# Layer 0 of a graph network: the first head's mask made earlier, its loads reordered, more layernorm buffers

## The chip, the cores and the metric

The kernel runs on one core of a Trainium2 chip (trn2). A core has five engines that run their own instruction queues: TensorE (PE in the profile; PEld is its weight load), VectorE (DVE), ScalarE (ACT), GpSimd (POOL) and SyncE (SP). They meet through semaphores. SP, ACT and POOL also issue DMAs, each from its own queue. The metric is the device time of one execution in microseconds, as a median of several runs.

## The reference

The network has 4096 nodes with 256 features, a dense 0/1 adjacency matrix, and four layers. Each layer is `x = layernorm(x + layer(x, adj))`. The change lies in layer 0, a graph attention layer with 8 heads of 32 channels:

```python
node_feats = (x @ W.T + b).reshape(num_nodes, num_heads, half)
logit_parent = (node_feats * a[None, :, :half]).sum(axis=-1)
logit_child = (node_feats * a[None, :, half:]).sum(axis=-1)
attn_logits = logit_parent[:, None, :] + logit_child[None, :, :]
attn_logits = jax.nn.leaky_relu(attn_logits, 0.2)
attn_logits = jnp.where(jnp.abs(adj_matrix)[..., None] != 0.0, attn_logits, 0.0)
attn_probs = jax.nn.softmax(attn_logits, axis=1)
out = jnp.einsum('ijh,jhc->ihc', attn_probs, node_feats)
...
x = _layernorm(x + _L0_gnn_ref(x, L0_gnn_W, L0_gnn_b, L0_gnn_a, adj), axis=-1)
```

A pair without an edge keeps logit 0 and so weight 1 in the softmax. Layers 1 to 3 (a product with the adjacency matrix, two steps of a sparsified attention, a mean over neighbours) are not touched by the change.

## The kernel before

The exponential of a leaky logit is a product: exp(p)·exp(c) where parent plus child logit is positive, and exp(0.2p)·exp(0.2c) elsewhere. So layer 0 needs three kinds of sums over the children j of a row i: over the edges with the 0.2 slope, over all nodes that are no edge, and, per head, a correction over those edges whose logit is positive. The first two do not depend on a sign and are one dense product for all heads. The third needs one 0/1 matrix per head.

`sums0` makes the features and the dense product. Its first loop takes pairs of 128-row blocks: it loads `x`, transposes it on PE (L450), copies it to `xT` (L452), multiplies by the weights (L456), and makes the features `nf`, the scaled features `v` and their two-part split `src` on DVE and ACT (L458 to L478). The logits of the parents go to DRAM as `lpd` (L469). `factors0` then finds bounds and writes the row factors `fac` and one integer, `fits`. Three `big` values come back through PE's last small product of that stage, and the PSUM space of the next stage becomes free behind them.

The second loop of `sums0` walks over steps of two row blocks (b = 0, 2, ... 30). In each step eight pieces `a` of the transposed adjacency matrix (2 x 4 blocks of 128x128, 512 KB) are loaded by SP into two buffers (L525). DVE casts a piece to `ar` (L527, two buffers), ACT makes bytes of it, `nb` (L530), which POOL stores to `nad` in DRAM (L531), and PE multiplies `ar` by `src` into `pz` (L537, 256 matmuls in a step). At a step's end DVE combines the sums to `zt`, and ACT issues the store to `zd` (L546 to L552). Between these, `factored` makes for each key block the factors `gb` of the heads, in three bf16 parts that DVE and ACT work out in turn, and stores them to `gmd` (L502 to L514). A scheduler sets the order of all this on each engine; it pulls the factors into the first third of the stage.

`chunk0` belongs to the head stage but is called in step b = 28. It makes the mask `gt0` for the first head and four key blocks over the first 1024 rows, from their stored bytes, with `na0` and `sg0` in the two `a` buffers (L246 to L253). Their factors are loaded to `gm0`.

`choose0` branches on `fits`: a general version of layer 0 follows that does not run on these inputs. All engines meet behind the branch.

The head stage takes two halves of four heads, and in each half four row groups of 1024 rows (`it`). So a head in it is one of 32 passes, each with 256 matmuls (L319): 32 key blocks in eight groups `g` of four, by eight row blocks. For each group a mask `gt` is made by `mask`. In groups 2, 5 and 7 DVE makes four comparisons of the broadcast parent logits `lpb` with a child's logit (L260) and one AND with the adjacency bytes `na` (L262); in the others ACT makes four sign activations (L266) and DVE one shift-and-AND (L268). `sg` has three buffers and `gt` four. At the start of a half SP loads `na` and `gm`, group by group:

```python
for g in range(NB // K):
    nc.sync.dma_start(na[:, g * K:(g + 1) * K], nad[it, :, g * K:(g + 1) * K, :])
    if it == 0 and (half or g):
        nc.sync.dma_start(gm[:, g * K:(g + 1) * K, 0], gmd[half, :, g * K:(g + 1) * K, 0])
```

POOL issues the loads of `lpb` and of `z` (from `zd`). At a head's end DVE reduces `acc` and normalizes it into `y` (L325 to L336). In the second half the row group's result is added to X by POOL (L350, L351), and its four pairs of blocks enter the list `later`. One of them is layernormed with each following head: the moments on DVE (L85, L86), the reciprocal root on POOL (L88, L89) and the last step on POOL too (L96). The pool `work` has two buffers of each tile unless it says otherwise, and so the layernorm's small tiles have two.

Of the kernel before, what the change touches and what calls it, by code (L numbers as in the profile page):

```python
# [9 lines left out]
F32 = mybir.dt.float32  # L10
I32 = mybir.dt.int32
F32R = mybir.dt.float32r
BF16 = mybir.dt.bfloat16
FP8 = mybir.dt.float8e4
U8 = mybir.dt.uint8
# [40 lines left out]
class Net:  # L56
# [17 lines left out]
        self.diag = pool.tile([P, self.NB], F32, name="diag")  # L74
        self.diagr = pool.tile([P, self.NB], F32R, name="diagr")

    def moments(self, pool, src):

        nc = self.nc
        n = src.shape[1]  # L80
        stats = pool.tile([P, n, nc.vector.BN_STATS_DIM], F32, name="ln_stats")
        mv = pool.tile([P, n, nc.vector.BN_AGGR_DIM], F32, name="ln_mv")
        rstd = pool.tile([P, n], F32, name="ln_rstd")
        for q in range(n):
            nc.vector.bn_stats(stats[:, q, :], src[:, q, :])  # L85
            nc.vector.bn_aggr(mv[:, q, :], stats[:, q, :])  # L86
        var = pool.tile([P, n], F32, name="ln_var")
        nc.gpsimd.tensor_scalar_add(var, mv[:, :, 1], EPS)  # L88
        nc.gpsimd.tensor_tensor(rstd, var, self.power.to_broadcast([P, n]), ALU.pow)  # L89
        return mv, rstd  # L90

    def layernorm(self, pool, dst, src, engine=None):

        mv, rstd = self.moments(pool, src)
        for q in range(src.shape[1]):
            (engine or self.nc.vector).tensor_scalar(dst[:, q, :], src[:, q, :], mv[:, q, 0:1], rstd[:, q:q + 1],  # L96
                                                     op0=ALU.subtract, op1=ALU.mult)
# [116 lines left out]
    def layer0(self):  # L214
# [7 lines left out]
        with ExitStack() as ctx:  # L222
# [10 lines left out]
            def row_logits(t, h, it):  # L233
                nc.gpsimd.dma_start(t, bass.AP(tensor=lpd.tensor, offset=lpd.offset + h * N + it * IT, ap=[[0, P], [1, IT]]))
                return t

            first = pool.tile([P, IT], F32, name="lpb0")
            gt0 = pool.tile([P, 4, IT], FP8, name="gt0")
            gm0 = pool.tile([P, 4, 6 * C1], BF16, name="gm0")


            nad = self.nad
# [1 line left out]
            yd = dram.tile([NB, P, D // 2], F32, name="yd")  # L244
            gmd = dram.tile([2, P, NB, H // 2, 6 * C1], BF16, name="gmd")

            def chunk0(work):

                nc.sync.dma_start(gm0, gmd[0, :, 0:4, 0])
                na0, sg0 = (work.tile([P, 2, 4, P], F32, name="a", bufs=2).rearrange("p q k i -> p (q k i)").bitcast(U8)  # L250
                            .rearrange("p (k i) -> p k i", k=4) for _ in range(2))
                nc.sync.dma_start(na0, nad[0, :, 0:4, :])
                mask(gt0, sg0.bitcast(FP8), na0, first, 0, 0)  # L253

            def mask(gt, sg, na, lpb, g, h):

# [11 lines left out]
                    nc.vector.scalar_tensor_tensor(bits[0], bits[1], SIGN_ABOVE, bits[2],  # L268
                                                   op0=ALU.logical_shift_right, op1=ALU.bitwise_and)

            self.sums0(both, nlc, fac, lpd, nad, zd, gmd, lambda: row_logits(first, 0, 0), chunk0)
            self.choose0(fac, zd, gmd, gm0)

            self.open_x()
# [11 lines left out]
            for half in range(2):  # L286
                for it in range(N // IT):
                    i0 = it * Q
                    for g in range(NB // K):
                        nc.sync.dma_start(na[:, g * K:(g + 1) * K], nad[it, :, g * K:(g + 1) * K, :])  # L290
                        if it == 0 and (half or g):
                            nc.sync.dma_start(gm[:, g * K:(g + 1) * K, 0], gmd[half, :, g * K:(g + 1) * K, 0])
                    for hh in range(1, H // 2 if it == 0 else 0):
                        for g in range(0, NB // K, 2):
                            nc.sync.dma_start(gm[:, g * K:(g + 2) * K, hh], gmd[half, :, g * K:(g + 2) * K, hh])
                    if half:
                        nc.sync.dma_start(X[:, i0:i0 + Q, :], xr[:, i0:i0 + Q, :])
                        y0 = work.tile([P, Q, D // 2], F32, name="y0", bufs=1)
                        nc.sync.dma_start(y0, yd[i0:i0 + Q].rearrange("b p d -> p b d"))
                    y = work.tile([P, Q, H // 2, C], F32, name="y")  # L300
                    for hh in range(H // 2):
                        h = half * (H // 2) + hh
                        lpb = row_logits(work.tile([P, IT], F32, name="lpb"), h, it) if h or it else first
                        z = work.tile([P, Q, C1], F32, name="z")
                        nc.gpsimd.dma_start(z, zd[i0:i0 + Q, :, h].rearrange("b p c -> p b c"))
                        acc = psum.tile([P, Q, 256], F32, name="acc")
                        for g in range(NB // K):

                            head0 = half == 0 and hh == 0 and g == 0
                            gt = gt0  # L310
                            if not head0 or it:
                                gt = work.tile([P, K, IT], FP8, name="gt", bufs=4)
                                sg = work.tile([P, K, IT], FP8, name="sg", bufs=3)
                                mask(gt, sg, na[:, g * K:(g + 1) * K, :], lpb, g, h)
                            for k in range(K):
                                jc = g * K + k
                                for q in range(Q):

                                    nc.tensor.matmul(acc[:, q, :6 * C1], gt[:, k, q * P:(q + 1) * P],  # L319
                                                     gm0[:, k, :] if head0 else gm[:, jc, hh, :],  # L320
                                                     start=(jc == 0 and q % 2 == 0),
                                                     stop=(jc == NB - 1 and q % 2 == 1))

                        red = work.tile([P, Q, 2 * C1], F32, name="red")
                        nc.vector.tensor_reduce(red, acc[:, :, :6 * C1].rearrange("p q (s c) -> p q c s", s=3),  # L325
                                                AX.X, ALU.add)

                        red = red.rearrange("p q (s c) -> p q s c", s=2)
                        nc.vector.tensor_mul(red, red, fac[:, 0:2, i0:i0 + Q, h].rearrange("p s q -> p q s").unsqueeze(3)
                                             .to_broadcast([P, Q, 2, C1]))  # L330
                        t1 = red[:, :, 0, :]
                        nc.vector.tensor_add(t1, t1, red[:, :, 1, :])
                        nc.vector.tensor_add(t1, t1, z)
                        r = work.tile([P, Q], F32, name="r")
                        nc.vector.reciprocal(r, t1[:, :, C])
                        nc.vector.tensor_mul(y[:, :, hh, :], t1[:, :, :C], r.unsqueeze(2).to_broadcast([P, Q, C]))  # L336
                        for xs in later[:per_head]:
                            self.layernorm(work, xs, xs, nc.gpsimd)
                        del later[:per_head]
                    y = y.rearrange("p q h c -> p q (h c)")  # L340
                    if not half:
                        nc.gpsimd.dma_start(yd[i0:i0 + Q].rearrange("b p d -> p b d"), y)
                        continue

                    if i0 + Q == NB:
                        self.add_w1()
                    engine = nc.vector if i0 + Q == NB else nc.gpsimd
                    for q in range(0, Q, 2):
                        xs = X[:, i0 + q:i0 + q + 2, :]
                        nc.gpsimd.tensor_add(xs[:, :, :D // 2], xs[:, :, :D // 2], y0[:, q:q + 2])  # L350
                        engine.tensor_add(xs[:, :, D // 2:], xs[:, :, D // 2:], y[:, q:q + 2])  # L351
                        later.append(xs)
# [47 lines left out]
        nc.vector.tensor_reduce(fits, lim.rearrange("p i h -> p (i h)"), AX.X, ALU.min)  # L400
        nc.scalar.dma_start(self.fits, fits)

    def sums0(self, both, nlc, fac, lpd, nad, zd, gmd, then, chunk0):

        nc, tc, NB, D, N = self.nc, self.tc, self.NB, self.D, self.N
        H, C = 8, 32
# [3 lines left out]
        with ExitStack() as ctx:  # L410
# [30 lines left out]
            bb = b0.to_broadcast([P, 2, D + 2 * H])  # L441
            for b in range(0, NB, 2):
                two = slice(b, b + 2)
                x = work.tile([P, 2, D], F32, name="x", bufs=3)
                nc.sync.dma_start(x, xr[:, two, :])
                px = ps.tile([P, 512], F32, name="ps_x", bufs=2)
                for c in range(2):
                    for q in range(2):
# [68 lines left out]
            for b in range(0, NB, 2):  # L517
# [2 lines left out]
                for q in range(2):  # L520
                    factored(b + q)
                for g in range(NB // G):
                    a = work.tile([P, 2, G, P], F32, name="a", bufs=2)
                    for q in range(2):
                        nc.sync.dma_start(a[:, q], self.adjt[b + q, :, g * G:(g + 1) * G, :])  # L525
                    ar = work.tile([P, 2, G, P], F32R, name="ar")
# [5 lines left out]
                    for q in range(2):  # L532
                        for k in range(G):
                            jc = g * G + k
                            for s in range(2):
                                for t in range(2):
                                    nc.tensor.matmul(pz[q][:, t, :W], ar[:, q, k, :], src[:, jc, t, s],  # L537
                                                     start=(jc == 0 and s == 0), stop=(jc == NB - 1 and s == 1))
                if b == NB - 4:
                    chunk0(work)  # L540
                for q in range(2):
                    zt = work.tile([P, 2, H, C1], F32, name="zt")
                    by_head = [t.rearrange("p (h c) -> p h c", h=H) for t in
# [5 lines left out]
                                            op0=ALU.mult, op1=ALU.add)  # L549
                    nc.vector.tensor_mul(zt[:, 1], zt[:, 1], of_row(3))  # L550
                    nc.vector.tensor_add(zt[:, 0], zt[:, 0], zt[:, 1])
                    nc.scalar.dma_start(zd[b + q], zt[:, 0])  # L552

    def general0(self, fac, zd, gmd, gm0):

# [1377 lines left out]
```

## Time and profile before

| what | us |
|---|---|
| median of three runs (4050.99 to 4052.44) | 4052.07 |
| the profiled execution | 4052.79 |
| its span, from the first to the last instruction | 4051.1 |
| opening of layer 0, until the first L537 | 0 to 72.0 |
| dense sums, L537 | 72.0 to 597.1 |
| branch | 597.1 to 602.8 |
| heads, L319 | 602.8 to 1326.5 |
| layers 1 to 3 | from 1326.5 on |

The mean granted clock of TensorE over the span is 0.986. In what follows, a row of the profile's groups reads: line, engine, operation, written tile <- read tiles, shape, count | busy time, mean ns of one | idle time of the engine just before them, and what ended it. A row of waits reads: who <- what ended it: total us, times, longest us. A row of a timeline has start, length, engine, line, operation and tiles, and in brackets the idle time before it with its releaser.

### The profile page before, as it was taken

What the parts mean: (1) busy time and instruction counts of PE and PEld (TensorE: products, weight loads), DVE (VectorE), ACT (ScalarE), POOL (GpSimd) and SP (SyncE); (2) the same over time, 40 slices, a digit from 0 to 9 for tenths busy, and PEclk for the clock granted to TensorE, in tenths of its full rate; (3) what the DMA queues carried; (4) which work ended last, traced back from release to release, by engine and by line L of the source; (5) the groups of instructions that cost most, each with busy time, mean ns of one, the idle gap of its engine ahead of it and who ended that gap; (6) DMA issues with size and microseconds to landing.
All of it is one profiled execution on the core that took longest, in us unless ns stands there. A gap on an engine that the chain in (4) does not pass through costs nothing. (4 is left out here: it accounts for less than half of the span.)

```text
span 4051.1 us, 68763 instructions
## 1 busy us (share of the span) xinstructions
PE 3914.2 (97%) x25081; PEld 3388.4 (84%) x25081; DVE 2994.8 (74%) x6643; ACT 2755.4 (68%) x5127; POOL 1076.8 (27%) x1322
## 2 busy tenths in 40 slices
PE   8999999999999999799999999999999999999899
PEld 7899999999999788468888888864888888888687
DVE  7643228999999444548787887847899999999364
ACT  5543339999998322358888888835888888888132
POOL 0111110111333122301111111113455555555211
PEclk9999999999999999899999999999999999999999
DMA  4765547334221596433233323363333333335541
GB/s 137 230 208 177 179 151 214 96 103 125 70 87 51 222 379 270 121 107 97 95 99 98 103 92 102 105 227 98 105 116 106 103 113 111 103 114 189 185 159 47
DMA packets 322442, 556.42 MB, mean 137 GB/s; under 512 B 72134, under 2 KB 148550, under 8 KB 317990
## 3 DMA queue, kind: packets, MB, share of 16 engines
q1 hardware_dynamic: 239920, 395.13, 30.1%
q0 software_dynamic: 27664, 84.44, 6.2%
q10 hardware_dynamic: 54502, 72.27, 5.2%
q8 instruction: 203, 3.33, 0.3%
q14 instruction: 153, 1.25, 0.1%
HBM read 385.78 MB, written 165.94 MB: 136 GB/s over the span
## 5 line engine op out<-in xcount | busy, mean ns | idle before, releaser
L1334 PE MATMUL ps_a<-X,aT 128*128 128x256 f32 x4096 | 970.5, 380 | 1.3 <-ACT h L1475 1.1
L1334 PEld LDWEIGHTS ps_a<-X,aT 128*128 128x128 f32 x4096 | 776.0, 190 | 125.5 <-issue 3.3
L319 PE MATMUL acc<-gm,gt 128*128 128x198 bf16 x8192 | 706.4, 249 | 23.0 <-DMA gm<-gmd 6.7
L319 PEld LDWEIGHTS <-gt 128*128 128x128 fp8e4 x8192 | 703.1, 98 | 26.3 <-issue 9.3
L266 ACT ACTIVATE sg<-lpb,nlc 128x1024 fp8e4<-128x1024 f32 x636 | 667.2, 1135 | 61.3 <-DVE gt L268 38.6
L179 PE MATMUL ps_r<-XD,adj_piece 128*128 128x512 f32 x1952 | 548.1, 416 | 5.3 <-DMA adj_piece<-adjs 5.2
L537 PE MATMUL pz<-src,ar 128*128 128x264 f32 x4096 | 511.3, 288 | 14.2 <-DVE ar L527 12.2
L537 PEld LDWEIGHTS pz<-src,ar 128*128 128x128 f32 x4096 | 507.7, 190 | 17.7 <-DVE ar L527 11.8
L1061 ACT ACTIVATE ja<-e,nc 128x2048 uint8<-128x2048 f32 x240 | 480.9, 2004 | 2.0
L1327 ACT COPY aT<-ps_tp 128x512 f32<-128x512 f32 x512 | 295.9, 578 | 228.3 <-PE ps_tp L1325 226.4
L179 PEld LDWEIGHTS ps_r<-XD,adj_piece 128*128 128x128 f32 x1952 | 346.1, 190 | 78.9 <-issue 13.4
L530 ACT ACTIVATE nb<-a 128x512 uint8<-128x512 f32 x256 | 156.5, 630 | 288.6 <-DMA a<-in_adjt_dram 279.7
L1126 DVE MAX8 cand<-v 128x8 f32<-128x256 f32 x1024 | 347.1, 411 | 4.4
L1176 DVE SCALAR_TENSOR_TENSOR e<-e,edge 128x512 f32<-128x512 f32 x512 | 347.2, 750 | 2.2
L1325 PE MATMUL ps_tp<-ident,e 128*128 128x128 f32 x2048 | 308.2, 273 | 0.0
L1122 DVE SCALAR_TENSOR_TENSOR v<-e,hi 128x2048 f32<-128x2048 f32 x128 | 301.4, 2355 | 2.4
L1325 PEld LDWEIGHTS ps_tp<-ident,e 128*128 128x128 f32 x2048 | 257.1, 142 | 50.9 <-issue 0.5
L968 PE MATMUL ps_logit<-kT,q 128*128 128x512 f32 x1024 | 278.0, 414 | 12.1 <-DVE kT L926 6.6
L260 DVE TENSOR_SCALAR sg<-lpb,nlc 128x1024 fp8e4<-128x1024 f32 x384 | 285.1, 778 | 5.9 <-DVEq L357 3.9
L970 ACT ACTIVATE e<-ps_logit 128x1024 f32<-128x1024 f32 x256 | 259.8, 1025 | 29.9 <-PE ps_logit L968 28.8
L527 DVE CAST ar<-a 128x1024 fp32r<-128x1024 f32 x128 | 88.6, 693 | 232.9 <-PE pz L537 231.9
L764 PE MATMUL ps_adj<-XD,adj_piece 128*128 128x512 f32 x1024 | 243.5, 398 | 0.0
(383 smaller groups left out, 5497.0 us busy)
## 6 DMA issues: line engine op xcount, KB each, us to landing
adj_piece<-adjs SPq DMA_DIRECT2D x552, 256.0 KB
a<-in_adjt_dram SPq DMA_DIRECT2D x256, 256.0 KB
adjs<-adj_piece SPq DMA_DIRECT2D x96, 512.0 KB
na<-nad SPq DMA_DIRECT2D x64, 512.0 KB
nad<-nb POOLq DMA_DIRECT2D x128, 128.0 KB, 3.4
lpb<-lpd POOLq DMA_DIRECT2D x32, 512.0 KB, 4.0
na<-nad ACTq DMA_DIRECT2D x16, 1024.0 KB
gmd<-gb ACTq DMA_DIRECT2D x64, 198.0 KB
```

Of the source, the lines that this page charges most:

```text
L179: nc.tensor.matmul(ps, a[:, k, :], rhs(jc).rearrange("p s d -> p (s d)"), start=(jc == 0), stop=(jc == self.NB - 1))
L260: nc.vector.tensor_scalar(sg[:, k, :], lpb, nlc[:, 4 * g + k, h:h + 1], 2.0 ** -5, op0=ALU.is_ge, op1=ALU.mult, saturate=False)
L266: nc.scalar.activation(sg[:, k, :], lpb, AF.Sign, scale=-1.0, bias=nlc[:, 4 * g + k, h:h + 1], saturate=False)
L319: nc.tensor.matmul(acc[:, q, :6 * C1], gt[:, k, q * P:(q + 1) * P], gm0[:, k, :] if head0 else gm[:, jc, hh, :], start=(jc == 0 and q % 2 ...
L537: nc.tensor.matmul(pz[q][:, t, :W], ar[:, q, k, :], src[:, jc, t, s], start=(jc == 0 and s == 0), stop=(jc == NB - 1 and s == 1))
L1061: nc.scalar.activation(ja, e[:, s * HALF:(s + 1) * HALF], f, bias=nc1, accum_out=fs[:, i + s:i + s + 1])
L1122: nc.vector.scalar_tensor_tensor(v, ec, hi, ec, op0=ALU.is_lt, op1=ALU.mult, accum_out=sb[:, s:s + 1])
L1126: nc.vector.max(cand[:, 8 * j:8 * j + 8], v[:, k * 256:(k + 1) * 256])
L1176: nc.vector.scalar_tensor_tensor(ec, ec, edge[:, j:j + 1], ec, op0=ALU.is_ge, op1=ALU.mult)
L1325: nc.tensor.transpose(pt[:, k * P:(k + 1) * P], e[:, jc * P:(jc + 1) * P], self.ident)
L1327: nc.scalar.copy(aT, pt)
L1334: nc.tensor.matmul(pa[:, :D], aT[:, k * P:(k + 1) * P], X[:, jc, :], start=(jc == 0), stop=(jc == NB - 1))
```

## The change

The mask of the first head is made for eight key blocks in place of four (`gt0` and `gm0` double), in four parts, each of two key blocks. The parts are called in steps b = 20 to 26; the scheduler, which orders by readiness, puts their instructions where their inputs are ready. Their scratch tiles are those named `nf` and `v`, which the first loop has left. All comparisons are DVE's, and a plain AND follows. For the space, the first loop's x goes through the two `a` buffers, four row blocks at a time. `gt0` is used in the first pass alone (before, its first group of factors also served the later row groups). The loads of `na` and `gm` begin with group 2 and end with groups 0 and 1 in that first row group. The last step's two `zd` stores are issued by SP. The layernorm's four small tiles get six buffers in the head stage.

```diff
-    def moments(self, pool, src):
+    def moments(self, pool, src, bufs=2):
...
-        stats = pool.tile([P, n, nc.vector.BN_STATS_DIM], F32, name="ln_stats")
+        stats = pool.tile([P, n, nc.vector.BN_STATS_DIM], F32, name="ln_stats", bufs=bufs)
...
-            gt0 = pool.tile([P, 4, IT], FP8, name="gt0")
-            gm0 = pool.tile([P, 4, 6 * C1], BF16, name="gm0")
+            gt0 = pool.tile([P, 8, IT], FP8, name="gt0")
+            gm0 = pool.tile([P, 8, 6 * C1], BF16, name="gm0")
...
-            def chunk0(work):
-
-                nc.sync.dma_start(gm0, gmd[0, :, 0:4, 0])
-                na0, sg0 = (work.tile([P, 2, 4, P], F32, name="a", bufs=2).rearrange("p q k i -> p (q k i)").bitcast(U8)
-                            .rearrange("p (k i) -> p k i", k=4) for _ in range(2))
-                nc.sync.dma_start(na0, nad[0, :, 0:4, :])
-                mask(gt0, sg0.bitcast(FP8), na0, first, 0, 0)
+            def early_mask(work, part):
+
+                if part == 0:
+                    nc.sync.dma_start(gm0, gmd[0, :, 0:8, 0])
+                two = slice(2 * part, 2 * part + 2)
+                na0, sg0 = (work.tile([P, 2, H, C1], F32, name=name).rearrange("p s h c -> p (s h c)")[:, :512]
+                            .bitcast(dt).rearrange("p (k i) -> p k i", k=2) for name, dt in (("nf", U8), ("v", FP8)))
+                nc.sync.dma_start(na0, nad[0, :, two, :])
+                for k in range(2):
+                    nc.vector.tensor_scalar(sg0[:, k, :], first, nlc[:, 2 * part + k, 0:1], 2.0 ** -5,
+                                            op0=ALU.is_ge, op1=ALU.mult, saturate=False)
+                bits = [t.rearrange("p k i -> p (k i)").bitcast(U32) for t in (gt0[:, two, :], sg0, na0)]
+                nc.vector.tensor_tensor(*bits, ALU.bitwise_and)
...
-                    for g in range(NB // K):
+                    begun = 2 if it == half == 0 else 0
+                    for g in [*range(begun, NB // K), *range(begun)]:
                         nc.sync.dma_start(na[:, g * K:(g + 1) * K], nad[it, :, g * K:(g + 1) * K, :])
-                        if it == 0 and (half or g):
+                        if it == 0:
                             nc.sync.dma_start(gm[:, g * K:(g + 1) * K, 0], gmd[half, :, g * K:(g + 1) * K, 0])
...
-                            head0 = half == 0 and hh == 0 and g == 0
-                            gt = gt0
-                            if not head0 or it:
+                            head0 = g < 2 and half == it == hh == 0
+                            if head0:
+                                gt = gt0[:, g * K:(g + 1) * K, :]
+                            else:
...
-                                                     gm0[:, k, :] if head0 else gm[:, jc, hh, :],
+                                                     gm0[:, jc, :] if head0 else gm[:, jc, hh, :],
...
-                            self.layernorm(work, xs, xs, nc.gpsimd)
+                            self.layernorm(work, xs, xs, nc.gpsimd, bufs=6)
...
-                x = work.tile([P, 2, D], F32, name="x", bufs=3)
-                nc.sync.dma_start(x, xr[:, two, :])
+                if b % 4 == 0:
+                    x4 = work.tile([P, 2, 4, P], F32, name="a").rearrange("p q k i -> p (q k i)").rearrange(
+                        "p (b d) -> p b d", d=D)
+                    for q in range(0, 4, 2):
+                        nc.sync.dma_start(x4[:, q:q + 2], xr[:, b + q:b + q + 2, :])
+                x = x4[:, b % 4:b % 4 + 2]
...
-                if b == NB - 4:
-                    chunk0(work)
+                if NB - 12 <= b < NB - 4:
+                    early_mask(work, (b - NB + 12) // 2)
...
-                    nc.scalar.dma_start(zd[b + q], zt[:, 0])
+                    (nc.sync if b == NB - 2 else nc.scalar).dma_start(zd[b + q], zt[:, 0])
```

More of the change, by code (lines that the diff above doesn't have):

```diff
@@ L75, in constants @@
         self.diagr = pool.tile([P, self.NB], F32R, name="diagr")
-    def moments(self, pool, src):
+    def moments(self, pool, src, bufs=2):
         nc = self.nc
         n = src.shape[1]
-        stats = pool.tile([P, n, nc.vector.BN_STATS_DIM], F32, name="ln_stats")
-        mv = pool.tile([P, n, nc.vector.BN_AGGR_DIM], F32, name="ln_mv")
-        rstd = pool.tile([P, n], F32, name="ln_rstd")
+        stats = pool.tile([P, n, nc.vector.BN_STATS_DIM], F32, name="ln_stats", bufs=bufs)
+        mv = pool.tile([P, n, nc.vector.BN_AGGR_DIM], F32, name="ln_mv", bufs=bufs)
+        rstd = pool.tile([P, n], F32, name="ln_rstd", bufs=bufs)
         for q in range(n):
@@ L86, in moments @@
             nc.vector.bn_aggr(mv[:, q, :], stats[:, q, :])
-        var = pool.tile([P, n], F32, name="ln_var")
+        var = pool.tile([P, n], F32, name="ln_var", bufs=bufs)
         nc.gpsimd.tensor_scalar_add(var, mv[:, :, 1], EPS)
@@ L90, in moments, with layernorm @@
         return mv, rstd
-    def layernorm(self, pool, dst, src, engine=None):
-        mv, rstd = self.moments(pool, src)
+    def layernorm(self, pool, dst, src, engine=None, bufs=2):
+        mv, rstd = self.moments(pool, src, bufs)
         for q in range(src.shape[1]):
@@ L269, in mask @@
                                                    op0=ALU.logical_shift_right, op1=ALU.bitwise_and)
-            self.sums0(both, nlc, fac, lpd, nad, zd, gmd, lambda: row_logits(first, 0, 0), chunk0)
+            self.sums0(both, nlc, fac, lpd, nad, zd, gmd, lambda: row_logits(first, 0, 0), early_mask)
             self.choose0(fac, zd, gmd, gm0)
@@ L401, in factors0, with sums0 @@
         nc.scalar.dma_start(self.fits, fits)
-    def sums0(self, both, nlc, fac, lpd, nad, zd, gmd, then, chunk0):
+    def sums0(self, both, nlc, fac, lpd, nad, zd, gmd, then, early_mask):
         nc, tc, NB, D, N = self.nc, self.tc, self.NB, self.D, self.N
@@ L522, in sums0 @@
                 for g in range(NB // G):
-                    a = work.tile([P, 2, G, P], F32, name="a", bufs=2)
+                    a = work.tile([P, 2, G, P], F32, name="a")
                     for q in range(2):
```

## The prediction

> **What bounds the kernel now.** I read the page first, then the waits of PE, then windows laid on the steps of the stages that the change touches, then timelines of the three places where these windows are too long. On the page:
>
> ```profile
> span 4051.1 us, 68763 instructions
> PE 3914.2 (97%) x25081; PEld 3388.4 (84%) x25081; DVE 2994.8 (74%) x6643; ACT 2755.4 (68%) x5127; POOL 1076.8 (27%) x1322
> L319 PE MATMUL acc<-gm,gt 128*128 128x198 bf16 x8192 | 706.4, 249 | 23.0 <-DMA gm<-gmd 6.7 <-DVE gt L262 5.8 <-ACTq L357 5.7
> ```
>
> TensorE sets the time nearly everywhere, so an edit is worth what it takes out of PE's few gaps and slow steps. Layer 0 has two stages with such gaps: the dense sums (L537, 72 to 597 us) and the heads (L319, 603 to 1326 us). One step of two row blocks of the dense sums is 256 matmuls; the windows below are laid on steps (columns: busy time of L537 on PE, granted clock, DMA share, GB/s).
>
> ```profile
> 140.60:177.90 37.30, 32.35 (x256) 1.00 0.66 216
> 246.10:277.50 31.40, 31.40 (x259) 1.00 0.56 185
> 528.40:562.90 34.50, 31.52 (x259) 0.99 0.46 156
> 562.90:597.10 34.20, 34.20 (x256) 0.91 0.40 131
> ```
>
> An undisturbed step takes 31.4 us. The steps b=2 to 8 take 34.8, 37.3, 35.0 and 33.2, because DVE and ACT make all the factors there. The steps b=28 and b=30 lose 3.1 and 2.8 us. The heads in the same way, one row per head of 256 matmuls:
>
> ```profile
> 602.80:636.00 33.20, 26.47 (x257) 0.79 1.04 298
> 636.00:657.80 21.80, 21.80 (x258) 1.00 1.07 289
> 1161.60:1188.80 27.20, 23.71 (x259) 0.94 0.04 8
> 1254.10:1282.80 28.70, 23.84 (x258) 0.94 0.08 24
> ```
>
> A free head takes 21.8 us. The first takes 33.2, and three after a row group's end take 24.5, 27.2 and 28.7: 15.0 us too much together. The causes, from the waits (total, times, longest) and the timeline:
>
> ```profile
> PE acc L319 <- DMA gm<-gmd: 6.7, 1, 6.7
> PE acc L319 <- ACTq L357: 5.7, 1, 5.7
> DVE ln_mv L86 <- POOL X L96: 10.1, 6, 2.3
> ```
>
> ```profile
> 552.88 4.27 ACT L266 ACTIVATE a<-lpb,nlc 128x1024 fp8e4<-128x1024 f32 x4 [3.72 <-DVE ar L527]
> 557.18 1.23 DVE L268 SCALAR_TENSOR_TENSOR gt<-a 128x1024 uint32<-128x1024 uint32 x1 [4.40 <-ACT a L266]
> 558.43 16.75 SPq L525 DMA_DIRECT2D a<-in_adjt_dram  x12
> 562.87 12.31 PE L537 MATMUL pz<-src,ar 128*128 128x264 f32 x77 [2.98 <-DVE ar L527]
> ```
>
> The mask of chunk 0 holds both `a` buffers until 558.4, so the next adjacency pieces are issued only then and PE stands for 2.98 us.
>
> **The change, part by part** (a minus is time saved).
>
> *The opening, 0 to 72 us: +1.2.* x now goes through the two `a` buffers, so no adjacency piece is fetched ahead. Before, two `ar` casts (0.69 us) fell into DVE's idle time at 14.7 to 16.0, and four `nb` copies (0.63 us) stood ahead of the first xT copy at 12.60, which let PE begin the features at 13.22. The weights were ready at 12.47, so 0.75 us come free, and about 0.5 more as the 128-byte loads of `a0` no longer share the engines with 1 MB of adjacency: -1.3. But now the order puts both casts and seven of the eight `nb` copies between the last four x pairs. DVE is busy 4.4 us of each 5 there, so 2 x 0.69 = +1.4. ACT is busy 3.5 of 5 and has some 3.6 us idle in four pairs (12.2 us) for 7 x 0.63 = 4.4, so +0.8, and I add 0.3 for the landing of the first piece. One new comparison stands before the copy `big` that releases PE, in the place of a 0.7 us operation that it pushes back: nothing. Ends -1 and +3.
>
> *The early mask in the dense sums: +3.5.* Eight comparisons (0.75 us, the L260 row) and four ANDs on half of L262's columns (about 0.6) are 8.4 us of DVE. Three further comparisons stand in step b=0, after `big`, where casts finish 2 to 3 us before PE needs them: hidden. Four comparisons and all ANDs stand in step b=6, and the loads of the adjacency bytes stand in SP's queue between the `a` pieces of that step. There, casts end 0.05 us before PE takes them, so nothing is hidden by lead. The first byte load waits for the store of that step's first piece (issued at 174.25 in this trace, 3.4 us to landing on the page), to 177.7; the next `a` piece was issued at 177.92 anyway, after its cast, so that wait is covered, but two 256 KB loads and their issue now lie ahead of the piece: 0.8 + 512 KB at the 350 GB/s that the queue reaches at 615 to 625, 1.5 us, hence +2.3. The third and fourth load each put 256 KB ahead of one piece (0.75). DVE's own 3.0 + 2.4 us there meet 8 us of DVE waits for ACT's `gb` in the step, so I charge about one AND. With overlap between these: +3.5. Ends 0 (the factor work is waiting for ACT anyway) and +8.4, plus the rival below. The doubled load of factors, 400 KB, goes out in step b=2 and waits for stores that land before the queue's next piece is due: 0.
>
> *Chunk 0 leaves step b=28: -5.9.* The two steps fall from 34.5 and 34.2 to 31.4. Here the Trainium skill, "TensorE: Matmul & The Clock Gate", section "What's actually happening", bears: it gives about 3.4 us of idling until the clock halves. This gap is 2.98 us, and still the clock row falls to 0.91 over the step that follows. By that figure only the gap, 3.1, would come back; by the windows 5.9. I take the windows.
>
> *The branch: -0.35.* ACT, which issued the last two `zd` stores and then loaded `fits`, reached the join at 602.74 and released PE at 602.80. With the stores on SP, ACT branches earlier and DVE, which is through at 602.33, is the last. SP has 0.6 us of waits after that and gains 0.3.
>
> *Head 0: -5.* With eight key blocks ready PE has 64 matmuls, some 7.5 us at the rising clock, instead of 4.6 us. Loads now begin with group 2. In this trace the bytes of group 1, second in the queue, were usable at 609.3 and its factors at 614.1; each further group lands 2.1 us after the last (727 KB at 350 GB/s). Now group 2 is usable near 607.5, group 3 near 614 (the POOL queue's lpb and z loads take half the rate from 607 to 613, and w1's 256 KB now goes first on ACT), the others at 2 us steps; so PE waits about 2 us once and ends the head near 628.3 instead of 636.0: -7.7 with the branch. But the masks of head 1 come only 3.4 to 4.3 us earlier: ACT saves one group, 4 x 1.06 us. In this trace a mask is ready 5.4 us before its first matmul at the start of head 1 and 0.8 in head 2, because DVE and ACT are both at 96% of a head. PE would catch up with the masks there, so I take about -5 beside the branch's 0.35. Ends -2.5 and -8. The byte loads of groups 0 and 1 moved to the end are needed by head 1 only, about 20 us later.
>
> *Six layernorm sets: -11.* After each row group, four layernorms of two blocks are interleaved with the masks on DVE, with two buffers each:
>
> ```profile
> 1160.14 4.93 POOL L96 TENSOR_SCALAR X<-X,ln_mv,ln_rstd 128x256 f32<-128x256 f32 x2
> 1165.10 0.18 DVE L86 BATCH_NORM_AGGREGATE ln_mv<-ln_stats 128x2 f32<-128x6 f32 x1 [1.04 <-POOL X L96]
> 1166.17 2.43 POOL L96 TENSOR_SCALAR X<-X,ln_mv,ln_rstd 128x256 f32<-128x256 f32 x2
> 1168.64 0.25 DVE L86 BATCH_NORM_AGGREGATE ln_mv<-ln_stats 128x2 f32<-128x6 f32 x2 [2.33 <-POOL X L96]
> ```
>
> DVE loses 3.4 us per row group, and the masks behind it starve PE. Call lead the time from a finished mask to the first matmul that takes it. It grows by 0.75 us in a free head. Over the two heads around 1161.6 it goes from 1.6 to 0.1 while PE is held up 5.4: DVE falls back by 1.5 + 5.4 + 1.5 = 8.4 us, without the waits by 5.0. The lead is 4.9 us before the first of the three stalls, so that one, 2.8 us, goes whole; it is about 2.4 at the two others, and each may keep 1.5 to 2.5 of 5.4 and 6.9. 15.0 - 4 = -11. A rule of the Trainium skill speaks against this: "SBUF — State Buffer", section "Who interferes with whom", says that a DVE instruction with two SBUF inputs and a GpSimd one that reads SBUF exclude each other, and the later blocks. DVE's masks would then wait at the port instead: six remaining L96 of 1.2 us each can hold it for 7 us, more than the 3.4 gained, and the part would be worth nothing or cost. In this trace the mask AND beside L96 took 1.20 us against 1.22 alone, while L96 stretched from 2.43 to 4.93: POOL pays. Only beside POOL's adds (L351) do comparisons take 1.2 instead of 0.75, and these stay as they are. I take -11, ends 0 and -13.
>
> Behind the heads every queue keeps its order, so the rest only moves. Sum: 1.2 + 3.5 - 5.9 - 0.35 - 5 - 11 = -17.6. The profiled execution took 4052.79 (span 4051.1 and 1.7 outside it), 0.7 over the median of 4052.07; I apply the sum to the median: 4034.5.
>
> **The rivals.** (1) The mask work is no limit and the early mask is hidden: head 0 gives 8 with the branch and b=6 costs 0, so 1.2 - 5.9 - 8 - 11 = -23.7: 4028. For it speaks the DVE idle time in step b=6; against it the shrinking lead in heads 1 and 2. Chance 0.15. (2) Costs at their upper ends: opening +3, b=6 +8.4, head 0 -2.5, all at once -8.4: 4043.7, two of them some -11 to -14. For it, no slack in b=6. Chance 0.19. (3) DVE meets POOL's port and the layernorm part is lost: -6.6, 4045.5. Chance 0.07. (4) Slower: in step b=6 SP's queue and DVE have no slack, and each of the four parts of the mask acts as chunk 0 did, with a stall near 3 us and half clock after it, 5.9 each, and 8.4 of DVE on top: 31.8 in place of 3.5, in all +10.7: 4063. It ends slower than before from a cost of 21.1 on. Against it: the store is awaited only to 177.7, before SP was free anyway. Chance 0.04. The main case has 0.55, with a range of its own of 4029 to 4040.
>
> **How the numbers follow.** A difference of about 0.2%, 8.1 us, is what can be told from no change. Faster by more: the main case, rival 1 and most of rival 2, 0.55 + 0.15 + 0.16 = 0.86. Same: the rest of rival 2, rival 3, 0.10. Slower by more: rival 4, 0.04. The range reaches from rival 1, with 3 us for the head parts' own bound, to rivals 2 and 3 at 4045.
>
> **What would show it.** Right: steps b=28 and 30 at 31.4 us; no wait of L86 on L96; head 0 near 25 to 28 us with a gap before group 3 instead of group 1; the three long heads below 25 us; step b=6 near 38.5; L537 beginning near 73. Wrong: step b=6 over 45 us or PE gaps over 3 us in it (rival 4); AND or comparison rows that grow beside L96 (rival 3); long heads 1 to 4 with the masks as releaser (the masks take back more of head 0 than I charge).

## The result, and the profile after

The changed kernel takes 4035.53 us (median of 6 runs, 4033.96 to 4040.32) against 4053.44 us (6 runs of the kernel before, the three shown earlier among them). The ratio is 0.9951, 95% interval 0.9938 to 0.9963, so it is faster by 15 to 25 us. The forecast was 4034.5. Its profiled execution took 4036.57 us, with a span of 4034.9. The page, in the lines that answer to those shown of before:

```profile
span 4034.9 us, 68768 instructions
PE 3907.4 (97%) x25081; PEld 3377.3 (84%) x25081; DVE 3000.8 (74%) x6653; ACT 2747.0 (68%) x5119; POOL 1086.8 (27%) x1322
L327 PE MATMUL acc<-gm,gt 128*128 128x198 bf16 x8192 | 701.0, 248 | 11.6 <-DVEq L365 5.3
```

PE's idle time ahead of the heads' matmuls has halved, from 23.0 to 11.6 us, and the largest part of what is left, 5.3 us, is the branch. Windows laid on the steps of the dense sums (columns: length, busy time of L549 on PE and on its weight loads, granted clock, DMA share, GB/s), first b=0 to 8, then b=10, 28 and 30:

```profile
73.80:107.20 33.40, 33.36 (x256) 33.39 (x257) 0.93 0.60 194
107.20:143.80 36.60, 33.72 (x259) 33.02 (x257) 0.95 0.72 232
143.80:182.80 39.00, 32.65 (x256) 31.58 (x256) 1.00 0.66 218
182.80:220.60 37.80, 33.66 (x257) 33.14 (x257) 0.95 0.71 235
220.60:255.30 34.70, 32.31 (x257) 31.54 (x257) 1.00 0.73 238
255.30:286.70 31.40, 31.40 (x259) 31.40 (x258) 1.00 0.60 193
537.60:568.90 31.30, 31.30 (x258) 31.30 (x257) 1.00 0.52 177
568.90:600.50 31.60, 31.55 (x258) 31.34 (x256) 1.00 0.37 120
```

Steps b=28 and 30 are free steps now, as forecast. But the steps b=2 to 8 have become longer, all four of them, and in b=2 and b=6 the clock dips to 0.95, where it was 1.00 before. Steps b=2 and 6 before (columns: length, busy time of L537 on PE, granted clock, DMA share, GB/s):

```profile
105.80:140.60 34.80, 32.30 (x258) 1.00 0.69 230
177.90:212.90 35.00, 32.69 (x256) 1.00 0.76 240
```

The windows of heads 0, 1, 25 and 29, with the busy time of L327:

```profile
605.80:633.70 27.90, 24.62 (x256) 23.66 (x257) 0.91 1.01 303
633.70:655.60 21.90, 21.89 (x257) 21.89 (x257) 1.00 1.16 286
1156.60:1179.70 23.10, 22.06 (x259) 21.82 (x257) 1.00 0.01 1
1245.30:1269.10 23.80, 22.07 (x259) 21.84 (x258) 1.00 0.01 1
```

Head 0 falls from 33.2 to 27.9 us, head 25 from 27.2 to 23.1, head 29 from 28.7 to 23.8. Head 21, which took 24.5, is now a free head of 21.9.

All kernels below are compared by such stages, from the first matmul of one to the first matmul of the next in the trace (us). "To head 1" runs from the end of the dense sums to head 1's first matmul; "behind" is what follows the heads, where no kernel of this table differs.

| kernel | dense sums begin | b=0 to 8 | b=28, 30 | to head 1 | heads 1 to 31 | heads end at | behind |
|---|---|---|---|---|---|---|---|
| before | 72.03 | 174.1 | 68.7 | 38.9 | 690.5 | 1326.5 | 2724.6 |
| changed | 73.84 | 181.5 | 62.9 | 33.3 | 679.3 | 1313.0 | 2721.8 |
| changed, second trace (`again`) | 73.96 | 180.2 | 62.9 | 33.7 | 679.4 | 1312.3 | 2724.2 |
| `six_sets` | 72.13 | 174.9 | 68.3 | 38.7 | 679.4 | 1315.6 | 2730.7 |
| `no_early` | 73.37 | 176.3 | 62.9 | 37.7 | 679.3 | 1311.8 | 2734.9 |
| `late` | 73.07 | 175.6 | 62.9 | 34.4 | 679.3 | 1307.5 | 2734.5 |
| `x_gt0` | 73.94 | 180.4 | 62.9 | 33.5 | 679.3 | 1312.3 | 2736.5 |
| `pool_load` | 72.98 | 180.1 | 62.9 | 32.4 | 679.4 | 1310.1 | 2732.0 |
| `old_order` | 72.11 | 181.3 | 62.9 | 39.7 | 679.4 | 1317.6 | 2730.6 |
| `paced` | 73.53 | 160.3 | 62.9 | 34.2 | 679.3 | 1292.5 | 2723.1 |
| `paced_late` | 73.19 | 159.2 | 62.9 | 33.5 | 679.7 | 1290.7 | 2730.9 |

The steps b=10 to 26 take 282.2 us in every one. The part behind varies by 15 us between traces of identical code there, so the whole time of one run says little, and the stages say much. Up to the heads' end the change is worth 1326.5 - 1313.0 = 13.5 us; the other 2.7 us of the first trace's 16.2 lie behind, where nothing was changed, and shrank to 0.4 in the second trace.

### The profile page after: what moved, and what is told of

Same layout as the page of the kernel before. It is cut to its first block, busy times and chain, and to the rows that moved or that the text cites. A ratio compares the mean times of both kernels' runs of the same rounds, so it can differ in the third digit from the quotient of the medians.

```text
span 4034.9 us, 68768 instructions
## 1 busy us (share of the span) xinstructions
PE 3907.4 (97%) x25081; PEld 3377.3 (84%) x25081; DVE 3000.8 (74%) x6653; ACT 2747.0 (68%) x5119; POOL 1086.8 (27%) x1322
## 5 line engine op out<-in xcount | busy, mean ns | idle before, releaser
L327 PE MATMUL acc<-gm,gt 128*128 128x198 bf16 x8192 | 701.0, 248 | 11.6 <-DVEq L365 5.3
L327 PEld LDWEIGHTS <-gt 128*128 128x128 fp8e4 x8192 | 698.9, 97 | 13.6 <-issue 8.0
L549 PE MATMUL pz<-src,ar 128*128 128x264 f32 x4096 | 510.9, 287 | 16.1 <-DVE ar L539 12.7
L549 PEld LDWEIGHTS pz<-src,ar 128*128 128x128 f32 x4096 | 507.6, 190 | 19.3 <-DVE ar L539 16.1
L980 PE MATMUL ps_logit<-kT,q 128*128 128x512 f32 x1024 | 276.9, 412 | 11.6 <-DVE kT L938 6.4
```

## The experiments

**The six layernorm sets alone (`six_sets`).**

```diff
 kernel before:
-                            self.layernorm(work, xs, xs, nc.gpsimd)
+                            self.layernorm(work, xs, xs, nc.gpsimd, bufs=6)
 (and bufs passed on to the four small tiles, as in the change)
```

> The kernel before with the six layernorm tile sets alone. My theory: the layernorm part is worth what the heads behind head 0 lost in the changed kernel, 690.5 - 679.3 = 11.2 us, wherever head 0 ends: about 4042, heads 21, 25 and 29 near 21.9, 23.1 and 23.8 us, no wait of the aggregation on POOL's scaling. Rival: part of those 11.2 us came from the masks' lead that the early mask left over, and the sets alone give 5 to 8: 4045 to 4048, with head 25 or 29 above 25 us.

Measured: 4047.04 us against 4059.48 for the kernel before, which ran beside it; ratio 0.9973 (0.9964 to 0.9982). The heads 1 to 31 take 679.4 us, as in the changed kernel to 0.1 us. This part gives its 11.1 us whatever head 0 does; the rival falls.

What of the rule on the shared port, which spoke against it? The groups by line from 1060 to 1300 us, POOL's scaling and DVE's AND, first before, then changed:

```profile
L96 POOL TENSOR_SCALAR X<-X,ln_mv,ln_rstd 128x256 f32<-128x256 f32 x24 | 50.3, 2101 | 1.3
L262 DVE TENSOR_TENSOR gt<-sg,na 128x1024 uint32<-128x1024 uint32 x31 | 37.6, 1214 | 0.8
```

```profile
L96 POOL TENSOR_SCALAR X<-X,ln_mv,ln_rstd 128x256 f32<-128x256 f32 x24 | 57.2, 2388 | 1.3
L268 DVE TENSOR_TENSOR gt<-sg,na 128x1024 uint32<-128x1024 uint32 x32 | 38.9, 1216 | 1.0
```

POOL's scaling got slower by 14%, the AND not at all, and the shift-and-AND of the other groups went from 1247 to 1255 ns. POOL pays, and nobody waits for it any longer: the wait of L86 on L96, 10.1 us before, no longer appears among DVE's waits.

**No layernorm in the heads (`no_ln`)**, to see what still makes heads 25 and 29 long.

```diff
-                        for xs in later[:per_head]:
-                            self.layernorm(work, xs, xs, nc.gpsimd, bufs=6)
                         del later[:per_head]
```

> The changed kernel without the interleaved layernorms in the heads (they are left out, so layer 1 reads X without them). From head 1 to the end of the heads 679.3 us with six sets; a free run is 31 heads of 21.78, 675.2. If DVE's own layernorm work (statistics) is what still starves PE in heads 25 and 29, all heads take 21.8 and the sum is 675 to 676; if it is the adds on POOL and DVE's work at a row group's end, heads 25 and 29 stay above 22.5.

Measured: heads 1 to 31 in 675.7 us, heads 25 and 29 at 21.9 each. The remaining 3.7 us are thus the layernorms' own work, not the adds at the row group's end. Which of its instructions cost them was not tried. (In this kernel and in `no_and` below, the layers behind work on other data and are not read.)

**No early mask (`no_early`)**, against two theories of the 7.4 us that the steps b=0 to 8 lost.

```diff
-                if NB - 12 <= b < NB - 4:
-                    early_mask(work, (b - NB + 12) // 2)
-                    begun = 2 if it == half == 0 else 0
+                    begun = 0
-                            head0 = g < 2 and half == it == hh == 0
+                            head0 = False
```

> The changed kernel without any mask made early: the dense sums hold no byte loads, comparisons or ANDs, and head 0 makes all its eight masks itself, with the loads in the order of groups 0 to 7. The steps b=0 to 8 of the dense sums took 174.1 us before and 181.5 in the changed kernel. Theory A (the early mask does that): 173 to 175 here. Theory B (the opening does it, because x through the a buffers delays the first pieces and the relay of DVE, ACT and PE starts from another place): 180 to 182 here. From the end of the dense sums to the end of head 0 there were 38.9 us before and 33.3 in the changed kernel; with nothing ready I expect 39 to 43. Time by A 4034 to 4038, by B 4041 to 4045.

Measured: 176.3 us in the steps b=0 to 8 (1.3 above the range of theory A, 3.7 below that of B), and 37.7 to head 1 instead of 33.3. So without the mask the dense sums get some 5 us back and head 0 loses 4.4. The heads end at 1311.8 against 1313.0 and 1312.3: where the change put it, the early mask brings nothing. The time, 0.9961 (0.9949 to 0.9974), fits that.

**The same mask in a late step (`late`).** The planner puts the mask where its scratch comes free. With `nf` and `v`, idle after the features, that is as soon as the bytes are stored, b=6. The `zt` tiles turn once per step, so there it is b=20 to 26, where the code stands.

```diff
-                            ... for name, dt in (("nf", U8), ("v", FP8)))
+                            ... for name, dt in (("zt", U8), ("zt", FP8)))
```

> The changed kernel with the scratch of the early mask taken from the zt tiles instead of nf and v, which come free two blocks per step only: its byte loads, comparisons and ANDs then fall into the steps b=20 to 26, where every cast is 3 us ahead of PE. Theory A (the early mask costs the steps b=0 to 8 their 7.4 us): these steps together 173 to 175 us, b=20 to 26 still 31.4 each, about 4028. Theory B (the opening does it): 180 to 182 us, time 4035. Rival C (a mask in a late step stalls as chunk 0 did, since its byte load waits in SP's queue for the zt tile): b=20 to 26 at 33 to 35 each, time 4035 to 4045.

Measured: 175.6 us in the steps b=0 to 8, 0.6 above theory A's range; the steps b=20 to 26, with four loads, eight comparisons and four ANDs in them, are at 31.36 each. Theory A holds, rival C falls. The casts end 3.0 us before PE takes them there; the mask's work takes this lead down to 1.1 us at the lowest, never to nothing, and so the whole early mask is free. The doubled load of factors stayed in step b=2 here (issued at 116.0), so it is not what costs. Ratio 0.9953 (0.9937 to 0.997); in the stages it is 5.5 us better than the changed kernel's first trace, less than the time can separate.

**x in another tile (`x_gt0`).**

```diff
-                    x4 = work.tile([P, 2, 4, P], F32, name="a").rearrange(...)
+                    x4 = gt0.rearrange("p k i -> p (k i)").bitcast(F32).rearrange("p (b d) -> p b d", d=D)[:, b % 8:b % 8 + 4]
```

> The changed kernel with x loaded into the quarters of gt0, which is idle until the masks, instead of the a buffers: adjacency pieces are fetched ahead of the features as before. First matmul of the dense sums at 72.03 before, 73.84 in the changed kernel; I expect 71.5 to 72.3, as the two casts and seven copies go back into idle time. Steps b=0 to 8: by theory A (early mask) still 180 to 182 us and the time 4033 to 4034; by theory B (opening) 174 to 176 and 4027 to 4029.

A miss for the opening: the dense sums begin at 73.94. The cast and copies are back at the start, but the first features begin at 15.65 us (11.68 in the changed kernel, 13.22 before), since PE waits 7.6 us for the first xT copy: ACT has four copies of adjacency pieces ahead of it again, and a fourth x pair is now loaded ahead of those pieces. What x in `a` costs at the end of the features, it had gained at their start. The steps b=0 to 8, at 180.4, again say theory A.

**Which part of the early mask costs?** Three kernels, one run each. Its byte loads on POOL's queue (`pool_load`), its comparisons left out (`and_only`), its ANDs left out (`no_and`, in which all eight comparisons move to step b=0):

```diff
 pool_load:
-                nc.sync.dma_start(na0, nad[0, :, two, :])
+                nc.gpsimd.dma_start(na0, nad[0, :, two, :])
 and_only:
-                for k in range(2):
-                    nc.vector.tensor_scalar(sg0[:, k, :], first, ...)
-                bits = [... for t in (gt0[:, two, :], sg0, na0)]
+                bits = [... for t in (gt0[:, two, :], na0, na0)]
 no_and:
-                    nc.vector.tensor_scalar(sg0[:, k, :], first, ...)
+                    nc.vector.tensor_scalar(gt0[:, 2 * part + k, :], first, ...)
-                nc.vector.tensor_tensor(*bits, ALU.bitwise_and)
```

> The changed kernel with the early mask's four byte loads issued by POOL instead of SP; comparisons and ANDs stay where they are. If the loads in SP's queue cost the step b=6 (my +2.3 and 0.75), the steps b=0 to 8 fall from 181.5 to 178 to 179 us; if it is DVE's work and its order (theory A by DVE), they stay at 181 to 182.

> The changed kernel without the early mask's eight comparisons: the adjacency bytes are ANDed with themselves, so head 0's first eight blocks lack the threshold; byte loads and ANDs stay where they were. Steps b=0 to 8 took 180.1 to 181.5 us with the whole early mask in the step b=6, 175.6 and 176.3 without. If the comparisons' 6 us of DVE cost most of it, 176 to 178 here; if the ANDs, which stand in DVE's queue behind byte loads, cost it, 179 to 181.

> The changed kernel without the early mask's ANDs: the comparisons write gt0 themselves (head 0's first eight blocks lack the adjacency) and stand in the step b=0, the four byte loads stay in SP's queue in the step b=6. If an AND in DVE's queue costs the 5 us of the early mask, the steps b=0 to 8 take 176 to 177.5 us; if the loads and what SP waits for do, 179 to 182, with b=6 at 38 or more; if it takes both, each alone leaves about half, 177.5 to 179.

Measured, steps b=0 to 8: 180.1, 182.2 and 185.9 us. None comes near 176, and with the ANDs left out the steps are even longer. So no part alone is shown to be the culprit. The comparisons do show in one place: step b=2 takes 35.2 to 35.7 us in the three kernels without comparisons in step b=0 (`late`, `no_early`, `and_only`) and 36.6 to 37.4 in the six that have three of the early mask's there (the changed kernel twice, `x_gt0`, `pool_load`, `old_order`, `no_ln`). I had costed them at nothing. But in `and_only` step b=6 rises to 40.9.

The queue that carries the byte loads (L254) stands still in either case: in the changed kernel SP waits 4.6 us for a store ahead of the first and 3.9 ahead of the third, in `pool_load` POOL waits 5.4 and 4.2 us for DVE ahead of two of them. That alone says little. SP's issues in the changed kernel, and the cast that frees the next buffer:

```profile
171.91 3.91 SPq L537 DMA_DIRECT2D a<-in_adjt_dram  x4
180.47 0.80 SPq L254 DMA_DIRECT2D nf<-nad  x2
182.86 0.81 SPq L537 DMA_DIRECT2D a<-in_adjt_dram  x2
```

```profile
182.10 0.69 DVE L539 CAST ar<-a 128x1024 fp32r<-128x1024 f32 x1
```

The next adjacency piece is issued at 182.86, right behind its cast, so the wait of 4.6 us ahead of the first two byte loads is covered, as forecast. Behind the third load the piece leaves 0.6 us after its cast.

These steps are a relay between DVE, ACT, the stores and PE, whose order the planner rewrites at every edit; the cost of the mask in it is the cost of the whole, and which wait carries how much of it stays open.

**The heads' loads in the old order (`old_order`).**

```diff
-                    begun = 2 if it == half == 0 else 0
+                    begun = 0
```

> The changed kernel with the heads' loads again in the order of groups 0 to 7. Groups 0 and 1 are then loaded first though head 0 doesn't need them, 1.45 MB or about 4 us. From the end of the dense sums to the start of head 1 33.3 us in the changed kernel; if loads bound head 0, 36 to 38 here, and if the masks do, 33 to 34.

The timeline of PE, first changed, then `old_order`:

```profile
605.75 8.02 PE L327 MATMUL acc<-gm,gt 128*128 128x198 bf16 x64 [5.30 <-DVEq L365]
615.50 2.88 PE L327 MATMUL acc<-gm,gt 128*128 128x198 bf16 x32 [1.73 <-DMA gm<-gmd]
619.48 13.77 PE L327 MATMUL acc<-gm,gt 128*128 128x198 bf16 x160 [1.10 <-DVE gt L274]
```

```profile
603.87 7.07 PE L327 MATMUL acc<-gm,gt 128*128 128x198 bf16 x64 [5.30 <-DVEq L365]
620.05 20.17 PE L327 MATMUL acc<-gm,gt 128*128 128x198 bf16 x213 [9.12 <-DVE gt L268]
```

39.7 us to head 1, beyond my 36 to 38 and longer than before the change: PE finishes the eight blocks and then stands for 9.12 us. Without the new order the early mask loses even its gain in head 0; the two are one edit.

**The changed kernel again, and the factor work spread (`again`, `paced`, `paced_late`).** The last two take the factor work's tile from the turning `zt` pair too, so that each step makes two blocks' factors; `paced` keeps the early mask as changed, `paced_late` has the late one.

```diff
-                v = work.tile([P, H, 2, C1], F32, name="vf")
+                v = work.tile([P, 2, H, C1], F32, name="zt").rearrange("p s h c -> p (s h c)").rearrange("p (h s c) -> p h s c", h=H, s=2)
```

> The changed kernel once more, to run on the same chip as the next kernel and to show how far its stages repeat. If the stages of layer 0 are set by the order of the instructions, all of them come out within 0.5 us of the first trace (dense sums from 73.8 to 600.5, head 1 to the end of the heads 679.3) and only the layers behind them differ; if chance sets them, steps b=2 to 8 or the opening differ by more than 1 us. Behind the heads the first trace was 2.7 us shorter than that of the kernel before, though nothing is changed there: I expect this difference to be chance, so not the same here.

> The changed kernel with the late mask, and with the factor work's vf tile taken from the zt tiles too, so that two blocks' factors are made per step instead of up to eight in the steps b=0 to 8. Theory A says that these steps are long, and an early mask dear in them, because all the factor work is pressed into them: then each falls to about 31.4 us, b=0 to 8 together to 158 to 162 (175.6 with the late mask alone), later steps stay at 31.4, and the time falls by about 14 us below that of the late mask, some 20 below the changed kernel. Rival C: the zt tiles become the wait (factors wait for the store of the step before), casts come late in every step, 32.5 us or more each, and the gain is lost or turned round.

> The changed kernel with the factor work taken from the zt tiles (two blocks per step), the early mask's scratch in nf and v as in the change, so that loads, comparisons and ANDs stay in the steps b=4 to 8. If the early mask costs only where the factor work leaves no lead, these steps stay at 31.4 us each and b=0 to 8 at 158 to 161; if it costs by itself (byte loads ahead of a pieces, ANDs ahead of casts), b=4 to 8 take 2 to 5 us more than the 94.1 of the late mask with spread factors.

`again`: heads 1 to 31 within 0.1 us of the first trace and head 0 within 0.5, as a fixed order would have it, but steps b=0 to 8 at 180.2, with single steps up to 1.7 us apart (b=8: 34.8 and 33.1). These steps are partly chance; the heads behind the first are not. Behind the heads the gain of 2.7 us shrank to 0.4, as expected. `paced_late`, steps b=0 and 2:

```profile
73.20:107.00 33.80, 33.80 (x257) 33.80 (x258) 0.92 0.46 154
107.00:138.30 31.30, 31.30 (x258) 31.30 (x257) 1.00 0.64 204
```

The steps b=4 to 8 are at 31.4 as well: every step from b=2 on is free, and rival C falls. On one chip `paced_late` took 4023.69 us (0.9911, 0.9895 to 0.9928) and the changed kernel 4042.38 (0.9967, 0.9955 to 0.9978), against 4058.04 before. It is the best of the versions that ran more than once. `paced` ran once (4017.28 us, against 4053.70 for the kernel before beside it), with steps b=4 to 8 at 31.36, 32.06 and 31.81, 1.2 us more than free. The same loads, comparisons and ANDs that cost some 5 us beside the factor work cost about 1 where that work is spread.

## Why the prediction was right

It was right in sign, size and most terms, and the median 4035.53 lies 1.0 us from it. Some of that closeness is luck. The stages give 13.5 us where 17.6 was forecast; the missing 4 us are the opening and the early mask, 1.8 + 7.4 in place of 1.2 + 3.5. The time came out near all the same, because the layers behind took 2.7 us less in the first trace without a cause in the change, and because the interval of the ratio is 10 us wide: in the later measurement (`again`) the medians lay 15.7 us apart and the ratio was 0.9967.

- *Layernorm sets, -11:* 11.1 with the sets alone and 11.2 with the rest. The three stalls, the lead that covers the first, and POOL as the one that pays at the port all hold. Rival 3 falls.
- *Chunk 0, -5.9:* 68.7 to 62.9, so 5.9. Taking the windows and not the gap alone was the right choice: the clock of the following step came back with the gap.
- *Head 0 with the branch, -5.35:* 38.9 to 33.3 and 33.7, so 5.2 to 5.6 (4.3 in `no_ln`, at 34.6). The branch alone went from 5.7 to 5.3, released by DVE, as forecast. PE waits 1.73 us ahead of group 2 and 1.10 ahead of group 3, where I had foreseen one wait of 2 at group 3. Heads 1 to 4 show no stall.
- *Opening, +1.2:* 1.8 in the first trace. The kernels that load x into `a` begin the dense sums at 72.1 to 74.0, the two with x in its own tiles at 72.03 and 72.13. First features came 1.54 us earlier (1.3 forecast). The last four pairs took 13.9 us in place of 12.4, which is about the two casts. Two things were not in the sum: a reduction (L377) that now stands behind the last pair's work and not ahead of it, 0.5, and one pair in the middle that took 4.6 us in place of 3.3. That pair is long in some kernels of the same opening and not in others (`old_order`, `no_ln`).
- *Early mask, +3.5:* the step that failed. The steps b=0 to 8 lost 7.4 us (6.1 in the second trace), near the upper end that I had given. The sums over these five steps (read the length and PE's busy time), for the kernel before, the changed kernel, `again` and `late`:

```profile
sum 174.10, PE 163.26 PEld 160.04 DVE 115.73 ACT 99.05 POOL 28.08; mean PE 32.65 PEld 32.01 DVE 23.15 ACT 19.81 POOL 5.62
sum 181.50, PE 165.70 PEld 162.67; mean PE 33.14 PEld 32.53
sum 180.22, PE 168.08 PEld 165.68; mean PE 33.62 PEld 33.14
sum 175.60, PE 165.25 PEld 162.48; mean PE 33.05 PEld 32.50
```

Length less busy time is PE's gaps: 10.8, 15.8, 12.1 and 10.4 us. So of the 7.4 us lost, 5.0 are longer gaps and 2.4 a slower clock in the same matmuls; of the 6.1 in the second trace, 1.3 and 4.8. Without a mask in these steps they take 175.6 and 176.3, against 174.1 and 174.9 with the old opening. As the gaps of all four are 10.4 to 11.1, the 1.5 between them lies in the clock, and is not shown to be a cost of the opening. Some 5 us belong to the mask.

Step b=6, which I had charged with nearly all of it, came near its forecast of 38.5, at 37.7 and 38.9. What was wrong is that the other steps and the clock were put at nothing: in the two traces b=2 grew by 1.7 and 2.0 us, b=4 by 1.8 and 0.4, b=8 by 1.6 and -0.2. The comparisons in step b=0 are not hidden by a lead of 2 to 3 us: step b=2 pays, probably because they push back the factor work. That term held nothing for a clock that falls behind the longer gaps. And a sum over single instructions is no price in a relay: no part of the mask carries it alone.

I had also read the -5 of head 0 and the +3.5 as separate gains and costs of a change that is worth 17; in truth they are one edit, and they cancel. The change lives from two parts alone: the six sets (11.2) and the removal of chunk 0 (5.9); without any early mask (`no_early`) the heads end at 1311.8, no later than with it. Rival 2 was nearest for the mask, but its three upper ends did not come together; rival 1 needed these steps to cost nothing, and rival 4 (its 31.8 should read 32.0) a step over 45 us, where the longest took 39.0.

## What to carry to other kernels

Work that is made ahead of time costs nothing only in a step where its engines have a lead, so read the lead (end of the producer to start of the consumer) step by step and put it there. Under a planner that issues work as soon as its tile is free, the choice of the scratch tile is the choice of the step: a tile that turns once per step paces the work, one that is idle early pulls it forward into the busiest part. And when an edit both gives and takes in neighbouring stages, sum them before calling it a gain.

## What was not expected of the hardware

The clock falls after shorter pauses than I had taken, and not each time. Two groups of 32 matmuls, the first after a gap of 1.90 us in the changed kernel, the second after 2.85 us in `x_gt0` (length, PE busy, granted clock):

```profile
122.20:127.70 5.50, 5.50 (x32) 0.69 0.76 232
```

```profile
182.10:186.00 3.90, 3.90 (x32) 1.00 0.87 247
```

In the traces of these steps, gaps of 1.75 to 2.86 us were followed by a group of about 5.4 us in place of 3.9 in some cases (about 6.7 once each in `again` and `no_ln`) and by an undisturbed one in others. The changed kernel has a gap of 2.85 us too, at 182.84, and there the group took 5.4. In the dense sums before, 1.65 and 2.37 us were both followed by 3.9. The Trainium skill, "TensorE: Matmul & The Clock Gate", section "What's actually happening", gives an idle window of about 3.4 us; here a gap of 1.90 sufficed. A group at half speed costs 1.5 us, so the two of them in the changed kernel cost 3.0 us (step b=0 took 0.4 less, hence the 2.4 above). A gap near 2 us should be priced with the chance of that on top.
